# Four convolution layers on one core: a coupled map in two halves of three channels instead of three pairs, with other orders of work around it

## The chip, the cores and the metric

The kernel runs on one core of a Trainium2 chip. The time is the device time of one execution, in microseconds (us). Three runs of the kernel before took 16,030.44, 16,057.42 and 16,071.58 us, median 16,057.42. One more execution was recorded by the hardware profiler.

The engines are named as the profile names them: PE (TensorE, matrix multiplications into PSUM), PEld (its weight loads), DVE (VectorE), ACT (ScalarE), POOL (GpSimd, which here issues DMAs), SP (SyncE, which issues DMAs too). DVE and ACT read PSUM and empty it.

## What is computed

The input is 32 pictures of 8 channels of 256 x 256 in float32. Four layers follow one another; each adds to x something computed from x normalized over groups of two channels (_gn).

```
drive = grid = gn(x)                                   # layer 0
for _ in range(15):                                    # "the map", "the automaton"
    mapped = 3.9 * grid * (1 - grid)
    local  = conv3x3(mapped, K_local, one kernel per channel)
    grid   = 0.85 * (0.7 * mapped + 0.3 * local) + 0.15 * drive
cml = clip(grid, 0.0001, 0.9999)
nca = sigmoid(conv1x1(relu(conv3x3(gn(x), Wp)), Wu))   # 8 -> 128 -> 8 channels
g   = sigmoid(conv1x1(relu(conv3x3([gn(x), cml, nca], Wg1)), Wg2))   # "the gate"
x   = x + g * cml + (1 - g) * nca
x   = x + conv3x3(quantized gn(x), quantized weight) / scales + bias     # layer 1
x   = x + conv3x3(gn(x), weight) + bias                                  # layer 2
x   = x + mean over 5x5 of gn(x), per channel                            # layer 3
```

## The kernel before, in words

**Layer 0 is one long pass over the 32 pictures.** Three generators are woven into one order of instructions by hand, in one loop: lattice() makes the map of one picture, errands() loads and normalizes the next picture, and gated() makes the hidden convolution and the gate. lattice() yields numbers, the "gaps"; the loop draws so much work from gated() as fills each gap (gated() yields what its pieces cost, in about the same unit), as long as the batch that gated() has reached (place[0]) stays under a cap (place[1]). The cap keeps the hidden convolution of a picture a few batches short of the point up to which its inputs are written: these are the batches held back, which are then drawn in the next picture's opening.

**The map.** Six of the eight channels (CP = 6) run on PE, the last two as nine shifted multiply-adds on DVE. For PE a channel lies as a tile of 128 partitions (16 blocks of rows x 8 columns within a block) by 512 elements. One step of one channel is two matmuls into one PSUM bank: `patch_sb` times the channel's state (L408), which covers the neighbours inside the patch, and `ring_sb` times `rings` (L410), which covers the neighbours beyond its border. `rings` is filled from the state by DMAs from SBUF to SBUF: spread() issues them on SP (L272). Then DVE adds the drive (L418), ACT squares the result into the state (L435), and the cycle begins again. ps_c holds three PSUM banks for these sums.

Before the change, channels go in pairs (j, 3 + j) for j = 0, 1, 2. The ring of a channel has 56 rows; the ring of the first of a pair lies on partitions 0 to 55 (LOW), that of the second on 64 to 119 (HIGH), so that two ring matmuls of 56 rows use different rows of the array. Two sets of tiles exist: pairs 0 and 1 are spread together after pair 1, pair 2 alone. A spread is 6 DMAs for each of the two sides, so 12; a step has 24.

The two channels on DVE lie in `strip`, 4 rows with one row above and below. tap(dy, dx) is one multiply-add of 128 x 1024 (L342), nine a step: two after pair 0, three after pair 1, four after pair 2, in the order dy = 1 first. Then L428 and L429 form the next values, and edges() fetches the rows above and below by two DMAs on SP (L278, L279). work(4) draws four of the gate's DVE operations (L603 to L612) from a list, `spare`, once a step; next(ahead) draws a piece of errands().

**The hidden convolution and the gate.** A batch is four matmuls `ph` of a 72-row input `im` (L684), each emptied by ACT into `hh` (L689), and four small matmuls `pn` (L661) which run side by side. A picture has 32 batches. `im` has four buffers; six DMAs on POOL (L540) fill one. The gate takes eight rounds a picture: POOL loads its inputs (L557, L494, L499, L562), PE makes eight matmuls of 128 x 128 and two of 72 x 32 (L571, L579, L583), ACT makes relu and sigmoid (L585, L590) with a matmul between them (L588), and DVE's seven operations go to `spare`. pieces() draws a stage of each gate at the end of each batch.

PSUM tiles of ph, of the small statistics (L109, L116, L138, L329), of the transposes (L366, L450) and of L588 share one ring of three banks.

**Layers 1 to 3** are a second pass, one picture at a time through all three: in one turn of its loop layer 3 of picture b - 3 runs first (eight parts, into which among() puts statistics, the quantization of picture b and the normalization normal2() of picture b - 1), then both() runs layer 2 of picture b - 1 and layer 1 of picture b, one part of each in turn. The copies beside() and beside3() (SP, L148, L860) bring rows of neighbouring blocks next to one another before the convolutions.

Of the kernel before, what the change touches and what calls it, by code (L numbers as in the profile page):

```python
# [17 lines left out]
P = 128  # L18
# [9 lines left out]
PW = 8  # L28
# [11 lines left out]
    (32, 8, (RB - 1) * PW, 1, -1, 1, 0),  # L40
    (40, 8, 0, 1, 1, 1, 0),
    (48, 2, (RB - 1) * PW, PW - 1, -1 - SY, 2, 2 * SY),
    (52, 2, 0, PW - 1, 1 - SY, 2, 2 * SY),
)
RING = 56
LOW, HIGH = 0, 64
# [3 lines left out]
PAIRS = CP // 2  # L50

SETS = ((0, 2), (2, 1))
RQ = 4
BLOCK = 12.6
# [17 lines left out]
def kernel(  # L72
# [59 lines left out]
    def by_group(psum, st):  # L132

        sel = small.tile([P, 4, 2], F32, name="sel")
        for j in range(2):
            nc.vector.tensor_scalar(sel[:, :, j], gsel_sb, st[:, j : j + 1], None, ALU.mult)
        ps = psum.tile([P, 512], F32, name="ps")
# [3 lines left out]
        return got  # L141
# [31 lines left out]
    with ExitStack() as es:  # L173
        wt = es.enter_context(tc.tile_pool(name="wt0", bufs=1))
        imp = es.enter_context(tc.tile_pool(name="im", bufs=4))
# [7 lines left out]
        ring_sb = const(wt, ring, [P, PAIRS, P], "ring_sb")  # L183
# [33 lines left out]
        for c in range(CP):  # L217
# [9 lines left out]
        states = [  # L227
            [wt.tile([P, k, SN], F32, name=f"state{i}_{side}") for side in range(2)]
            for i, (_, k) in enumerate(SETS)
        ]  # L230
        rings = [wt.tile([P, k, SN], F32, name=f"rings{i}") for i, (_, k) in enumerate(SETS)]
# [6 lines left out]
        for t in (*states[0], *states[1], *rings):  # L238
            nc.gpsimd.memset(t, 0.25)
# [15 lines left out]
        def inner(c):  # L255

            side, j = divmod(c, PAIRS)
            i = j // 2
            return states[i][side][:, j - SETS[i][0], AT : AT + TX * SY].rearrange(
                "p (x y) -> p x y", y=SY  # L260
            )[:, :, 0:TY]

        def spread(i):

            long = (SETS[i][1] - 1) * SN + RN
            to = rings[i].rearrange("p c n -> p (c n)")
            for state, base in zip(states[i], (LOW, HIGH)):
                row = state.ap[0][0]
                for q, n, p, step, far, m, by in RINGS:
                    at = p * row + AT + far  # L270
                    dims = [[step * row, n]] + ([[by, m]] if m > 1 else []) + [[1, long]]
                    nc.sync.dma_start(  # L272
                        to[base + q : base + q + n * m, 0:long], window(state, at, dims)
                    )
# [57 lines left out]
        def lattice(b, ahead):  # L332
# [67 lines left out]
            for step in range(STEPS):  # L400
                for j in range(PAIRS):
# [22 lines left out]
                    for dy, dx in taps_of[j]:  # L424
                        tap(dy, dx)
# [679 lines left out]
```

## Time and profile before

| | |
|---|---|
| median of three runs | 16,057.42 us (16,030.44 to 16,071.58) |
| the profiled execution | 16,044.26 us |
| its span in the profile | 16,042.5 us |
| PE busy | 15,001.2 us, 94% |
| DVE busy | 11,572.5 us, 72% |
| ACT busy | 5,754.6 us, 36% |
| POOL busy | 5,667.6 us, 35% |
| DMA: bytes and mean rate | 2,248.19 MB, 140 GB/s |
| mean granted clock of PE | 0.96 of full speed |
| layer 0 | to about 13,200 us |
| layers 1 to 3 | from about 13,320 us on |

How to read it: a line of PE's groups has line, engine, operation, tiles, shapes and count, then busy time and mean ns of one, then idle time of the engine just before these instructions and what ended it. A line of the timeline has start, duration, engine, line, operation, count, and in brackets the idle time before it with its releaser. A float32 matmul stands as two records, so L408 has 32 x 15 x 6 x 2 = 5,760. Matmuls overlap and their ends are modelled: the pace of PE is read from start to start, not from durations.

### The profile page before, as it was taken

To read this page: it belongs to the slowest core of one execution; us is meant where nothing else is said; L and a number is where in the kernel's file an instruction comes from. 1 tells how busy PE (TensorE), PEld (TensorE's weight loads), DVE (VectorE), ACT (ScalarE), POOL (GpSimd) and SP (SyncE) were. 2 spreads that over 40 slices of the span, in tenths; PEclk is the share of its full clock that TensorE was granted. 3 is DMA by queue.
4 is the path that set the end of the run, shared out by engine and by line. 5 is a ranking of instruction groups with operands and counts; after the bars stand their busy time and mean duration, and the time that the engine had idled before them with its cause. 6 is when DMAs were issued, how large, how long until landed. Compare 5 with 4: busy or idle time off the path is not lost. (4 is left out here: it accounts for less than half of the span.)

```text
span 16042.5 us, 158554 instructions
## 1 busy us (share of the span) xinstructions
PE 15001.2 (94%) x42888; PEld 5437.6 (34%) x42888; DVE 11572.5 (72%) x14652; ACT 5754.6 (36%) x8864; POOL 5667.6 (35%) x9558
## 2 busy tenths in 40 slices
PE   7999999999999999999999999999999997999999
PEld 2333333333333333333333333333333333333333
DVE  7777777777777777777777777777777775555554
ACT  3444444444434444444434444444444431111110
POOL 3433333333433433334433333333333332111111
PEclk9999999999999999999999999999999998999999
DMA  5666666666666666666666666566656554555554
GB/s 128 149 148 148 148 146 144 146 147 147 149 146 145 150 144 148 147 147 150 146 144 145 143 146 148 141 149 145 146 145 145 142 143 106 119 117 119 120 118 106
DMA packets 1172088, 2248.19 MB, mean 140 GB/s; under 512 B 472477, under 2 KB 676373, under 8 KB 1164949
## 3 DMA queue, kind: packets, MB, share of 16 engines
q0 software_dynamic: 734208, 1628.10, 42.8%
q1 hardware_dynamic: 437012, 609.95, 15.8%
q8 instruction: 370, 6.06, 0.2%
q14 instruction: 498, 4.07, 0.1%
HBM read 1169.35 MB, written 539.02 MB: 106 GB/s over the span
## 5 line engine op out<-in xcount | busy, mean ns | idle before, releaser
L342 DVE SCALAR_TENSOR_TENSOR acc<-strip,taps_sb,acc 128x1024 f32<-128x1024 f32 x3840 | 4925.9, 1283 | 485.2 <-DMA strip<-strip 387.4
L540 POOL DMA_DIRECT2D im<-xn_d x6144 | 3483.8, 573 | 4640.2 <-PE ph L684 3775.8
L684 PE MATMUL ph<-im,wp_sb 72*128 72x512 f32 x8192 | 4269.2, 635 | 269.3 <-ACT hh L689 126.5
L689 ACT ACTIVATE hh<-ph,bp_sb 128x512 f32<-128x512 f32 x4096 | 2758.0, 688 | 3778.2 <-PE ph L684 3726.1
L418 DVE SCALAR_TENSOR_TENSOR psc<-psc,flat 128x512 f32<-128x512 f32 x2880 | 1871.5, 693 | 2524.4 <-PE psc L410 2517.8
L408 PE MATMUL psc<-state,patch_sb 128*128 128x512 f32 x5760 | 2931.1, 623 | 163.0 <-ACT state L435 157.6
L435 ACT ACTIVATE state<-psc,minus 128x512 f32<-128x512 f32 x2688 | 1723.7, 689 | 3137.9 <-DVE psc L418 2756.2
L684 PEld LDWEIGHTS ph<-im,wp_sb 72*128 72x128 f32 x8192 | 1439.8, 195 | 2677.8 <-issue 1971.7
L410 PE MATMUL psc<-rings,ring_sb 56*128 56x512 f32 x5760 | 1805.7, 650 | 230.9 <-DMA rings<-state 212.6
L408 PEld LDWEIGHTS psc<-state,patch_sb 128*128 128x128 f32 x5760 | 1041.7, 194 | 1904.1 <-issue 1249.6
L871 PE MATMUL psv<-xr,w_sb 128*128 128x512 f32 x2560 | 1163.0, 600 | 1.3 <-DVE xr L852 1.3
L661 PE MATMUL pn<-hh,wu_sb 128*32 128x512 f32 x8192 | 1138.1, 624 | 0.0
L836 POOL DMA_DIRECT2D x_d<-x x512 | 324.9, 650 | 1944.5 <-DVE x L830 1703.1
L410 PEld LDWEIGHTS psc<-rings,ring_sb 56*128 56x128 f32 x5760 | 485.4, 187 | 1436.0 <-issue 1037.1
L571 PE MATMUL pg<-cq,wg_sb 128*128 128x512 f32 x1536 | 772.8, 642 | 0.0
L785 PE MATMUL psv<-xh,w_sb 128*128 128x512 f32 x1536 | 750.1, 627 | 9.6 <-issue 9.6
L571 PE MATMUL pg<-xq,wg_sb 128*128 128x512 f32 x1536 | 741.7, 620 | 0.0
L814 ACT ACTIVATE x<-psv,b_sb,sc 128x512 f32<-128x512 f32 x256 | 199.0, 777 | 1461.6 <-PE psv L789 1440.9
L562 POOL DMA_DIRECT2D xc<-xr_d x256 | 145.7, 569 | 1554.5 <-DVE ext L603 673.2
L871 PEld LDWEIGHTS psv<-xr,w_sb 128*128 128x128 f32 x2560 | 466.1, 189 | 610.9 <-issue 606.0
L342 DVE SCALAR_TENSOR_TENSOR acc<-strip,taps_sb,d 128x1024 f32<-128x1024 f32 x480 | 612.4, 1276 | 0.0
L891 DVE TENSOR_TENSOR y<-psv,y 128x512 f32<-128x512 f32 x256 | 177.1, 692 | 591.8 <-PE psv L871 591.8
(165 smaller groups left out, 12207.9 us busy)
## 6 DMA issues: line engine op xcount, KB each, us to landing
im<-xn_d POOLq DMA_DIRECT2D x6144, 96.6 KB, 4.4
rings<-state SPq DMA_DIRECT2D x1920, 70.1 KB
strip<-strip SPq DMA_DIRECT2D x960, 126.0 KB
rings<-state SPq DMA_DIRECT2D x1920, 35.1 KB
xn_d<-xb POOLq DMA_DIRECT2D x128, 516.0 KB, 11.3
nh_d<-nh POOLq DMA_DIRECT2D x256, 258.0 KB, 5.4
nr_d<-xb POOLq DMA_DIRECT2D x128, 516.0 KB, 7.0
xq<-nr_d POOLq DMA_DIRECT2D x128, 516.0 KB, 5.7
```

The lines of the kernel that those rows point to most:

```text
L342: nc.vector.scalar_tensor_tensor(acc, strip[:, dy : dy + RQ, dx : dx + W], taps_sb[:, 3 * dy + dx : 3 * dy + dx + 1], d2 if dy == 1 and dx ...
L408: nc.tensor.matmul(pss[-1], patch_sb[:, c, :], inner(c), start=True, stop=False)
L410: nc.tensor.matmul(ps, ring_sb[base : base + RING, j, :], rings[i][base : base + RING, j - SETS[i][0], 0 : TX * SY].rearrange("p (x y) -> ...
L418: nc.vector.scalar_tensor_tensor(ps, ps, FLOOR, dr[:, c], ALU.max, ALU.add)
L435: nc.scalar.activation(inner(c), ps, AF.Square, bias=minus)
L540: nc.gpsimd.dma_start(im[24 * dy : 24 * dy + 24, k, 0:run], window(xn_d[b % 3], at, [[HP * WP, C], [1, 3], [1, run]]),)
L571: nc.tensor.matmul(o, wg1_sb[:, s, dx, :], src[:, :, dx : dx + W], start=s == dx == 0, stop=False,)
L661: nc.tensor.matmul(pn[32 * q : 32 * q + 32, :], wu_sb[:, i, :], hh, start=i == 0, stop=i == 3,)
L684: nc.tensor.matmul(ph.rearrange("p (k w) -> p k w", w=W), wp_sb, im[:, :, j * WP : j * WP + W], start=True, stop=True,)
L689: nc.scalar.activation(hh, ph, AF.Relu, bias=bp_sb)
L785: nc.tensor.matmul(o, w[:, dx, :], src[:, 2 * i : 2 * i + 2, dx : dx + W], start=dx == 0, stop=False,)
L871: nc.tensor.matmul(pss[k].rearrange("p (c w) -> p c w", w=W), w3_sb[:, dx, :], xr[:, k, mine, dx : dx + W], start=dx == 0, stop=stop,)
```

## The change

It has five parts.

1. **The map in halves.** Channels 0 to 2 and 3 to 5 form two halves. Each half has one state tile and one `rings` tile. A half makes three patch matmuls, then three ring matmuls; the ring has 80 rows instead of 56 (the two DMAs of each edge and its corners become one DMA of 24 rows that overlap in the source) and is no longer placed in two row groups of the array. spread() issues 4 DMAs a half, 8 a step. Taps: the three of dy = 1 in half 0, the six of dy = 0 and 2 in half 1. work(4) stands in half 0, follow() in half 1. The gaps become 1.7 and 4.5 a half.
2. **Batches held back.** The cap lies five, not four, under the end of the picture; for the first picture it is raised only after its first squares, and a gap after the first spread is 8 instead of 5.5.
3. **Buffers and the place of the gate.** `im` has three buffers instead of four and is loaded three batches ahead instead of four; pieces() runs after the second matmul of a batch instead of at its end.
4. **Layers 1 to 3.** The steps of the statistics of layer 1 stand at parts 0, 1, 1, 2 of layer 3 instead of 0 to 3, and normal2() at part 2 instead of 3; those of layer 2 stand one part later; by_group() is split, DVE's part at part 4 and PE's at part 6, instead of both at 5; the quantization stands at parts 0, 2, 2, 3, its copy beside() at 3 instead of 4. both() starts layer 1 two parts after layer 2 and finishes it alone.
5. **Clearing.** Of the tiles cleared ahead of layer 1, DVE clears only the borders or the small ones, and POOL one (xr2), where POOL cleared six whole tiles.

The diff, cut to its core:

```diff
-    (32, 8, (RB - 1) * PW, 1, -1, 1, 0),
-    (40, 8, 0, 1, 1, 1, 0),
-    (48, 2, (RB - 1) * PW, PW - 1, -1 - SY, 2, 2 * SY),
-    (52, 2, 0, PW - 1, 1 - SY, 2, 2 * SY),
+    (32, 8, (RB - 1) * PW, 1, -1 - SY, 3, SY),
+    (56, 8, 0, 1, 1 - SY, 3, SY),
 )
-RING = 56
-LOW, HIGH = 0, 64
+RING = 80
...
-        imp = es.enter_context(tc.tile_pool(name="im", bufs=4))
+        imp = es.enter_context(tc.tile_pool(name="im", bufs=3))
...
-        ring_sb = const(wt, ring, [P, PAIRS, P], "ring_sb")
+        ring_sb = const(wt, ring, [RING, CP, P], "ring_sb")
...
+        def spread(half):
+
+            long = (HALF - 1) * SN + RN
+            state = states[half]
+            row = state.ap[0][0]
+            to = rings[half].rearrange("p c n -> p (c n)")
+            for q, n, p, step, far, m, by in RINGS:
+                at = p * row + AT + far
+                dims = [[step * row, n]] + ([[by, m]] if m > 1 else []) + [[1, long]]
+                nc.sync.dma_start(to[q : q + n * m, 0:long], window(state, at, dims))
...
-                    place[1] = BATCHES * (b + 1) - (4 if b + 1 < B else 1)
+                        place[1] = BATCHES * (b + 1) - (5 if b + 1 < B else 1)
...
-            yield 5.5
-            taps_of = (((1, 0), (1, 1)), ((1, 2), (0, 0), (0, 1)), ((0, 2), (2, 0), (2, 1), (2, 2)))
+            yield 8
             for step in range(STEPS):
-                for j in range(PAIRS):
-                    i = j // 2
-                    mine = (j, PAIRS + j)
+                for half in range(2):
+                    mine = range(HALF * half, HALF * half + HALF)
...
-                    for dy, dx in taps_of[j]:
-                        tap(dy, dx)
+                    for dy in (1,) if half == 0 else (0, 2):
+                        for dx in range(3):
+                            tap(dy, dx)
...
-                    yield 0.8
+                    yield 1.7
                     if step < STEPS - 1:
-                        for c, ps in zip(mine, pss):
-                            nc.scalar.activation(inner(c), ps, AF.Square, bias=minus)
-                        if j == SETS[i][0] + SETS[i][1] - 1:
-                            spread(i)
-                        if end:
+                        for c in mine:
+                            nc.scalar.activation(inner(c), pss[c % HALF], AF.Square, bias=minus)
+                        spread(half)
+                        if half == 1:
                             edges()
-                    if end:
+                    if half == 0:
                         work(4)
                     else:
-                        next(ahead, None)
-                    if j == 1:
                         follow()
-                    yield BLOCK - 4.0 if end else 0.8
+                    next(ahead, None)
+                    yield BLOCK - 1.7
...
                         if j == 1 and late:
                             second()
                             yield 1.05
+                        if j == 1:
+                            yield from pieces(batch)
                         yield 0.87
...
-                    yield from pieces(batch)
                     batch += 1
-                    coming = load(n + 1, i) if n + 1 < B * NCH else iter(())
+                    ahead = divmod(batch + 2, 4)
+                    coming = load(*ahead) if ahead[0] < B * NCH else iter(())
...
-                    for _ in layer2(b - 1, x2s[b - 1], bns[1]) if 1 <= b <= B else range(8):
-                        next(ones_, None)
+                    twos = layer2(b - 1, x2s[b - 1], bns[1]) if 1 <= b <= B else iter(range(8))
+                    for i, _ in enumerate(twos):
+                        if i > 1:
+                            next(ones_, None)
                         yield
+                    for _ in ones_:
+                        pass
```

BLOCK, the sum of a half's two gaps, is 6.2; before, a step's gaps summed to 12.6.

## The prediction

> **What bounds the kernel now.** I read the page's busy table, the table by stretch of the span, TensorE's groups, the waits, and the timeline of single steps. First, the busy table and two stretches (columns: stretch, PE, PEld, DVE, ACT, POOL busy, granted clock, DMA share, GB/s):
>
> ```profile
> PE 15001.2 (94%) x42888; PEld 5437.6 (34%) x42888; DVE 11572.5 (72%) x14652; ACT 5754.6 (36%) x8864; POOL 5667.6 (35%) x9558
> 4000.00:8000.00 4000.00, 3784.99 (x11025) 1329.06 (x11021) 3027.74 (x3563) 1637.58 (x2546) 1587.12 (x2720) 0.96 0.61 147
> 13600.00:15800.00 2200.00, 2068.16 (x5447) 865.65 (x5446) 1268.26 (x2315) 287.21 (x378) 359.98 (x511) 0.98 0.52 119
> ```
>
> TensorE is the bound in both parts. Layer 0 lasts to about 13,200 us (412 a picture). There TensorE is idle 786 us (13,200 less the busy time of the stretches, 12,414). A mean clock of 0.96, where the records know only 0.5 and 1.0, is 8% of the time at half speed, so 4%, 530 us, is lost. Idle and half clock cost 1,316 us, **41 us a picture**. Next, TensorE's groups in layer 0 and two waits of layers 1 to 3:
>
> ```profile
> L684 PE MATMUL ph<-im,wp_sb 72*128 72x512 f32 x8192 | 4269.2, 635 | 269.3 <-ACT hh L689 126.5 <-ACT gt L590 103.2 <-DMA im<-xn_d 21.4
> L408 PE MATMUL psc<-state,patch_sb 128*128 128x512 f32 x5760 | 2931.1, 623 | 163.0 <-ACT state L435 157.6 <-DVE flat L421 2.3 <-DMA strip<-strip 0.5
> L410 PE MATMUL psc<-rings,ring_sb 56*128 56x512 f32 x5760 | 1805.7, 650 | 230.9 <-DMA rings<-state 212.6 <-issue 17.4 <-DMA im<-xn_d 0.5
> L138 PE MATMUL ps<-sel,ones 128*128 128x8 f32 x64 | 12.6, 270 | 45.5 <-DVE sel L136 45.5
> L789 PE MATMUL psv<-qb,w_bf 72*128 72x512 bf16 x256 | 101.4, 396 | 123.1 <-DMA qb<-qh 123.1
> ```
>
> A matmul is two records. L408 and L410 have the same count and mean, but L410 is busy 1,806 instead of 2,931 us: the rings of two channels run side by side. The timeline shows the pace from start to start:
>
> ```profile
> 4006.28 2.74 PE L571 MATMUL pg<-xq,wg_sb 128*128 128x512 f32 x6
> 4008.86 1.88 PE L408 MATMUL psc<-state,patch_sb 128*128 128x512 f32 x4
> 4010.67 1.13 PE L410 MATMUL psc<-rings,ring_sb 56*128 56x512 f32 x4
> 4011.73 1.13 PE L588 MATMUL pq<-g,wg_sb 128*128 128x512 f32 x2
> ```
>
> Six plain records take 2.58 us, 0.43 each; the four of a ring pair take 1.06. The pair's surroundings pay too: 1.81 for four L408 instead of 1.72, and L588's two take 0.96 (next start 4012.69) instead of 0.86.
>
> Where the 41 us arise, by two places of the timeline. At each picture's start the rings come late, and what follows runs at half speed (3.78 us for four records):
>
> ```profile
> 4147.25 1.12 PE L410 MATMUL psc<-rings,ring_sb 56*128 56x512 f32 x2
> 4154.69 2.04 PE L410 MATMUL psc<-rings,ring_sb 56*128 56x512 f32 x2 [6.32 <-DMA rings<-state]
> 4156.66 3.78 PE L684 MATMUL ph<-im,wp_sb 72*128 72x512 f32 x4
> ```
>
> And inside the steps VectorE waits for the two edge rows of its strip, ScalarE for VectorE, TensorE for PSUM that ScalarE has not emptied:
>
> ```profile
> 3856.45 2.60 DVE L342 SCALAR_TENSOR_TENSOR acc<-strip,taps_sb,acc 128x1024 f32<-128x1024 f32 x2 [5.66 <-DMA strip<-strip]
> 3862.13 1.29 ACT L435 ACTIVATE state<-psc,minus 128x512 f32<-128x512 f32 x2 [10.93 <-DVE psc L418]
> 3864.05 3.78 PE L684 MATMUL ph<-im,wp_sb 72*128 72x512 f32 x4 [5.66 <-ACT gt L590]
> ```
>
> The waits give VectorE 387 us in 140 such stops.
>
> **What the Trainium skill says.** "TensorEngine Tiling (Array Packing)", Key Properties: tiles work in parallel, and "Changing tiling mode (not just tile) drains the TensorE". The trace agrees: 1.06 us for two ring matmuls, about 0.2 us lost around each pair. "TensorE: Matmul & The Clock Gate", What's actually happening: an idle window of about 3.4 us halves the clock; the trace shows it after the 6.32 us. The same page, Architectural detail: ScalarE and VectorE are strict first-in first-out; the chain above shows it. "DMA: Bandwidth & Descriptors", Issuing engines are not separate DMA queues: all queues share 16 engines, so larger ring transfers compete with POOL's loads (0.61 busy now); no run shows yet by how much.
>
> **The change, part by part.**
>
> *Unpacked rings.* Now one pair costs 4 x 0.43 + 0.09 + 1.06 + 0.10 = 2.97 us, three pairs 8.9 a step. After it, 80 rows need the whole array: 6 channels x 4 records x 0.43 = 10.3, without switches. That is +1.4 us in each of 15 x 32 = 480 steps: **+670**, fully on the path. Bounds: +620 (a switch costs 0.03 more than I read) to +810 (the 0.10 behind each pair is not won back).
>
> *Fewer ring DMAs.* SP issues 24 a step at 0.69 us (13.15 us for 19) and 2 strips, 18 us of a 22 to 24 us step; after it 8 and 2, some 7. Rows grow from 2 x 56 x (4.5 + 2.2 KB) to 2 x 80 x 6.8 KB, 0.75 to 1.09 MB a step, +160 MB on the page's 2,248: DMA share +0.04. The first half is ready after 3 squares and 4 issues instead of 4 and 12: 0.6 + 8 x 0.69 = 6 us sooner, and its rings are used 2.5 us later (waits of 8 instead of 5.5). The 6.3 us go, with the half clock behind them. A second half waits for 3 more squares and 4 issues, 4.7 us, and is used 11 us later: nothing, unless the transfers slow down.
>
> *Halves, centre row first.* Taps dy=1 need no edge rows and now stand in half 0; edge rows are used only in half 1, about 11 us after their issue instead of 4. The 5.66 us was a landing some 8 us after issue, so nearly all 387 us go. What comes late next is VectorE itself: half 1 has 3 x 0.61 + 6 x 1.31 + 0.72 + 1.17 = 11.6 us, half 0 has 1.8 + 3.9 + four helper operations of 0.71 = 8.6, and 0.7 a step of statistics: 20.9, of which a normal step of TensorE (10.3 + 12.4 of other work) hides all: 22.7. Where a gate flushes four more (2.8 us), VectorE is 1 to 3 us over. A half's three PSUM banks are needed 6.2 + 5.1 us after its start; VectorE then has 2 us of slack. I take 4 us a picture, bounds 0 and 15.
>
> *Amounts held back and gaps.* The gaps that lattice() yields sum to 222.8 instead of 223.3 a picture (5 + 8 + 3 + 4.8 + 8 + 15 x 12.4 + 8), so the other work of TensorE is moved, not changed. One more batch is left for the turn of pictures, 8 ph records and 8 pn records, about 4.5 us: cost nothing, since it only changes place; without it the transposes there would wait bare for VectorE and ScalarE.
>
> *Three input buffers instead of four, gates amid a batch.* The lead of a load in the built program's order falls from 34 to 23 us at the median. Moved past on POOL: the gate's 10 to 13 DMAs (0.57 us each) with their wait for VectorE. In the trace of before, 77 of 1,020 loads landed later than one batch before their use, 378 us in sum; as loads now precede the gate in the queue, I take 2 us a picture, bounds 0 and 12.
>
> *Left per picture:* 4 + 2, 1.5 for small statistics matmuls (L116 in the steps now), 3 at the turn of pictures, and half clock in the present proportion (530 to 786), some 4: **15 instead of 41**, -26 x 32 = **-830**. Bounds 8 and 26.
>
> *Layers 1 to 3.* Layer 1 begins two rounds (about 7 us) later and its edge copy a round earlier, against a wait of 123/32 = 3.8 us: gone. The group sums are split: 45 us mostly gone. With the half clock of these waits (0.98: 2% of half speed, 1% of 2,700, some 30 to 50 us) and the start, where POOL clears tiles for 20 us before it loads: **-200**, bounds -90 and -280. Two tail rounds of layer 1 cost VectorE 1.4 us each, hidden by layer 3's first 3.4 us of matmuls.
>
> **Sum.** 16,042.5 + 670 - 830 - 200 = 15,683 of span; the profiled run is 1.8 above its span, and the median of the runs 13 above that: **15,700**.
>
> **Rivals.** Differences under 0.3% (48 us) can't be told from none.
> - *Forecast*, 8 to 23 us left per picture: 15,480 to 15,950. Chance 0.55.
> - *Nearly no stall* (5 us left, -10 x 32): 15,380. For: SP and strip waits have a clear cause. Against: gates are bursts. 0.12.
> - *Only the picture starts heal* (about 27 left: some 4 us of rings, some 7 of half clock, little else goes): 15,700 + 12 x 32 = 16,080, spread 15,950 to 16,200. For: ScalarE stays behind VectorE. 0.16.
> - *Loads late* (the full 12 us a picture instead of 2, +320, and up to as much half clock again): 16,020 to 16,340. For: POOL was blocked by a gate in the late cases. Against: the queue's new order. 0.05.
> - *Slower: VectorE's half 1.* If its chunk exceeds TensorE's 11.4 us by more than the 2 us of slack, the squares come late, the banks are not free and TensorE stops in each step. At 1 us a step the picture's rest is 30 instead of 15 and the time 16,180; if all 41 us stay, it is 16,530. It decides from 26 us left on. For: 92% occupancy of VectorE. 0.12.
>
> Faster: 0.55 + 0.12 + 0.05 of the third; same 0.10 (0.08 and 0.02); slower 0.18. The range reaches down into the second case and up to the third and the edge of the last: 15,400 to 16,150.
>
> **What would show it.** L410: records 0.43 apart, busy near 2,900, no wait over 50 us in all; no first-ring wait; DVE's wait for strip under 60; L684's waits for ScalarE under 130; L789 and L138 without theirs; granted clock 0.97 to 0.98 in layer 0; about 407 us from picture to picture. It is wrong if L408 waits for L435 or DVE is over 92% busy in the steps, or L684 waits for im.

## The result, and the profile after

The kernel after took **16,744.57 us** (median of four runs, 16,739.85 to 16,758.92), the kernel before, beside it, 16,047.08 (four runs, 16,030.44 to 16,071.58). The ratio is **1.0444**, 95% interval 1.0429 to 1.0459: 698 us slower. The forecast was 15,700, its range ended at 16,150. The profiled execution has a span of 16,757.1 us, 714.6 above that of before.

First the busy table of the kernel after, from the page:

```profile
PE 15639.5 (93%) x42888; PEld 6260.4 (37%) x42888; DVE 11671.5 (70%) x14662; ACT 5733.7 (34%) x8864; POOL 5673.7 (34%) x9551
```

Then two stretches, one in layer 0 and one in layers 1 to 3 (columns as before: stretch, five engines, granted clock, DMA share, GB/s):

```profile
4000.00:8000.00 4000.00, 3712.95 (x10175) 1471.78 (x10174) 2842.16 (x3321) 1497.60 (x2351) 1452.46 (x2494) 0.93 0.64 146
14400.00:16500.00 2100.00, 2068.80 (x5556) 867.17 (x5554) 1269.63 (x2359) 292.95 (x382) 384.56 (x516) 1.00 0.61 128
```

Layer 0 went wrong: PE stands still more (287 us in the 4,000 instead of 215) and its clock is 0.93 instead of 0.96. Layers 1 to 3 went as meant: 1.00 instead of 0.98. The groups of PE name the new wait:

```profile
L668 PE MATMUL ph<-im,wp_sb 72*128 72x512 f32 x8192 | 4151.9, 633 | 789.4 <-DMA im<-xn_d 568.1 <-ACT hh L673 142.0 <-DVE xb L437 47.0
L393 PE MATMUL psc<-state,patch_sb 128*128 128x512 f32 x5760 | 2722.6, 609 | 32.2 <-ACT state L421 21.2 <-DVE flat L407 11.0
L395 PE MATMUL psc<-rings,ring_sb 80*128 80x512 f32 x5760 | 2635.3, 592 | 5.7 <-DMA rings<-state 5.7
L783 PE MATMUL psv<-qb,w_bf 72*128 72x512 bf16 x256 | 98.1, 383 | 10.9 <-DMA qb<-qh 10.9
L134 PE MATMUL ps<-sel,ones 128*128 128x8 f32 x64 | 9.3, 218 | 11.2 <-DVE sel L131 11.2
```

The waits that the change aimed at are gone: for `rings` 5.7 us instead of 212.6, for the squares (L421) 21.2 instead of 157.6, for `qb` 10.9 instead of 123.1. In their place L668, the hidden convolution, waits 568.1 us for its input `im`, which was 21.4 before. It happens at the same place in each picture, its opening. The timeline of PE there (start, duration; in brackets the idle time before; cut at the dots), and below it the busy time and granted clock of a stretch after the first stop:

```profile
4317.15 1.88 PE L668 MATMUL ph<-im,wp_sb 72*128 72x512 f32 x4
4324.39 3.75 PE L668 MATMUL ph<-im,wp_sb 72*128 72x512 f32 x4 [5.36 <-DMA im<-xn_d]
...
4343.80 3.75 PE L668 MATMUL ph<-im,wp_sb 72*128 72x512 f32 x4 [9.67 <-DMA im<-xn_d]
...
4407.23 3.75 PE L668 MATMUL ph<-im,wp_sb 72*128 72x512 f32 x4 [9.25 <-DMA im<-xn_d]
```

```profile
4324.39:4330.94 6.55, 6.55 (x13) 1.85 (x14) 0.00 (x0) 4.46 (x7) 5.03 (x8) 0.50 0.83 165
```

There are three stops in this picture, 24 us, and after each the same four records take 3.75 us instead of 1.88: the clock is halved (0.50 in the stretch shown). These are batches 29 and 30 of the picture that ends and batch 2 of the next; over all pictures they stop PE for 149, 239 and 169 us. What POOL, which issues the loads, does in the same time:

```profile
4302.50 4.06 POOL L343 DMA_DIRECT2D xn_d<-xb  x4 [16.75 <-DVE xb L337]
4306.56 2.24 POOL L524 DMA_DIRECT2D im<-xn_d  x4
4311.41 0.56 POOL L524 DMA_DIRECT2D im<-xn_d  x1 [2.61 <-DMA xn_d<-xb]
4314.68 0.56 POOL L524 DMA_DIRECT2D im<-xn_d  x1 [2.71 <-DMA xn_d<-xb]
4320.80 0.60 POOL L602 DMA_DIRECT2D x_d<-xc  x1 [5.55 <-DMA xn_d<-xb]
4325.37 0.56 POOL L546 DMA_DIRECT2D xc<-xr_d  x1 [3.97 <-DMA x_d<-xc]
4325.93 1.70 POOL L524 DMA_DIRECT2D im<-xn_d  x3
4327.63 2.77 POOL L462 DMA_DIRECT2D cr_d<-xb  x4
4332.14 0.58 POOL L524 DMA_DIRECT2D im<-xn_d  x1 [1.74 <-DMA xc<-xr_d]
```

POOL waits 16.75 us for DVE to normalize the next picture (L337), issues four stores of 516 KB, and after four more DMAs each further one waits for one of these stores to land, although the loads read another picture's tile. The built program's order on POOL shows why (rows in order, cut at the dots, with the semaphores that each waits for):

```
2167 L343 DMACopy xn_d_203<-xb_173 8x16x1032 [waits DMASW2_49,DVE_49]
2168 L343 DMACopy xn_d_203<-xb_173 8x16x1032 [waits DMASW3_49]
2169 L343 DMACopy xn_d_203<-xb_173 8x16x1032 [waits DMASW4_49]
2170 L343 DMACopy xn_d_203<-xb_173 8x16x1032 [waits DMASW5_49]
2171 L524 DMACopy im<-xn_d_202 24x1x1030 [waits DMASW6_49,PE_49]
...
2175 L524 DMACopy im<-xn_d_202 24x1x1030 [waits DMASW2_49]
2176 L524 DMACopy im<-xn_d_202 24x1x1030 [waits DMASW3_49]
2177 L602 DMACopy x_d_81<-xc 128x512 [waits DMASW4_49]
2178 L546 DMACopy xc<-xr_d_204 128x512 [waits DMASW5_49,DMASW4_49]
```

POOL's DMAs take eight semaphores in turn, so each waits until the one eight places ahead of it has landed. The fifth load DMA after four stores waits for the first store, the sixth for the second, x_d for the third: the brackets of the timeline, one by one. A store landed 11.1 us after its issue at the median, a load DMA 5.8. So POOL has at most eight transfers in flight, and four large ones hold up what comes eight places later.

For batch 30 these waits count: those of the timeline sum to 14.8 us before its first DMA is issued (at 4325.93), 10.9 of them for stores. For batch 29 they don't: the first four DMAs of its load were issued without a wait and yet landed 14.4 to 15.0 us after their issue (medians over the pictures; 2.8 to 3.5 for batches 27 and 28), and the last two, which had waited, landed only 0.5 us after them. That load is late because it stands behind stores that wait for DVE, and then because its transfers take so long beside theirs. The order by semaphores is the same in the kernel before, but there the loads of batches 28 to 30 are issued ahead of the stores and land 2.8 to 7.5 us after issue.

### The profile page after: what moved, and what is told of

The parts are those of the page before. It is cut to its first block, busy times and chain, and to the rows that moved or that the text cites. A ratio compares the mean times of both kernels' runs of the same rounds, so it can differ in the third digit from the quotient of the medians.

```text
span 16757.1 us, 141212 instructions
## 1 busy us (share of the span) xinstructions
PE 15639.5 (93%) x42888; PEld 6260.4 (37%) x42888; DVE 11671.5 (70%) x14662; ACT 5733.7 (34%) x8864; POOL 5673.7 (34%) x9551
## 5 line engine op out<-in xcount | busy, mean ns | idle before, releaser
L668 PE MATMUL ph<-im,wp_sb 72*128 72x512 f32 x8192 | 4151.9, 633 | 789.4 <-DMA im<-xn_d 568.1
L404 DVE SCALAR_TENSOR_TENSOR psc<-psc,flat 128x512 f32<-128x512 f32 x2880 | 1939.6, 696 | 3564.5 <-PE psc L395 3561.9
L393 PE MATMUL psc<-state,patch_sb 128*128 128x512 f32 x5760 | 2722.6, 609 | 32.2 <-ACT state L421 21.2
L395 PE MATMUL psc<-rings,ring_sb 80*128 80x512 f32 x5760 | 2635.3, 592 | 5.7 <-DMA rings<-state 5.7
L668 PEld LDWEIGHTS ph<-im,wp_sb 72*128 72x128 f32 x8192 | 1561.9, 199 | 2789.9 <-issue 2054.3
L421 ACT ACTIVATE state<-psc,minus 128x512 f32<-128x512 f32 x2688 | 1696.9, 690 | 1641.4 <-DVE psc L404 1441.1
L393 PEld LDWEIGHTS psc<-state,patch_sb 128*128 128x128 f32 x5760 | 1106.5, 195 | 1557.2 <-issue 1475.9
L395 PEld LDWEIGHTS psc<-rings,ring_sb 80*128 80x128 f32 x5760 | 1091.4, 190 | 1397.9 <-issue 1385.7
L645 PE MATMUL pn<-hh,wu_sb 128*32 128x512 f32 x8192 | 1268.8, 674 | 6.6 <-ACT hh L673 6.6
L830 POOL DMA_DIRECT2D x_d<-x x512 | 374.4, 746 | 1394.8 <-DVE x L824 1172.2
L415 DVE SCALAR_TENSOR_TENSOR strip<-acc 128x1024 f32<-128x1024 f32 x448 | 549.7, 1227 | 15.3
## 6 DMA issues: line engine op xcount, KB each, us to landing
xn_d<-xb POOLq DMA_DIRECT2D x128, 516.0 KB, 11.1
```

What stands on the lines that cost most here:

```text
L393: nc.tensor.matmul(pss[-1], patch_sb[:, c, :], inner(c), start=True, stop=False)
L395: nc.tensor.matmul(pss[c % HALF], ring_sb[:, c, :], rings[half][:, c % HALF, 0 : TX * SY].rearrange("p (x y) -> p x y", y=SY)[:, :, 0:TY], ...
L404: nc.vector.scalar_tensor_tensor(ps, ps, FLOOR, dr[:, c], ALU.max, ALU.add)
L421: nc.scalar.activation(inner(c), pss[c % HALF], AF.Square, bias=minus)
L645: nc.tensor.matmul(pn[32 * q : 32 * q + 32, :], wu_sb[:, i, :], hh, start=i == 0, stop=i == 3,)
L668: nc.tensor.matmul(ph.rearrange("p (k w) -> p k w", w=W), wp_sb, im[:, :, j * WP : j * WP + W], start=True, stop=True,)
```

## The experiments

Below, *turn* is the time from the first tap of a picture's last step to the first tap of the next picture (mean of 31), *steps* that of the 14 steps before it (mean of 32), *tail* what follows the last of these taps, and *stops* the idle time of PE, in sum, before batches whose load of `im` landed at the end of it. (The start of the kernel is left out, so that before has 6 here and 21.4 in the group above; the groups name only the last wait, so they can differ from this column by some 20 us.) All are from the traces. Times are medians; each ratio is to runs of the kernel before on the same chip. Kernels that ran on different occasions are compared by their ratios, a hundredth being 160 us.

| kernel | us | ratio, 95% interval | turn | steps | tail | stops |
|---|---|---|---|---|---|---|
| before | 16,047 | 1 | 71.3 | 339.8 | 2,869 | 6 |
| after | 16,745 | 1.0444 (1.0429 to 1.0459) | 93.6 | 344.8 | 2,727 | 582 |
| after_im3s | 16,657 | 1.0367 (1.0348 to 1.0386) | 91.9 | 342.2 | 2,725 | 556 |
| after_im4 | 16,089 | 1.0021 (1.0013 to 1.0028) | 78.9 | 338.2 | 2,724 | 123 |
| after_hold3 | 16,280 | 1.0130 (1.0108 to 1.0152) | 87.1 | 336.1 | 2,711 | 322 |
| after_gates_end | 16,457 | 1.0236 (1.0216 to 1.0257) | 91.0 | 337.0 | 2,722 | 515 |
| after_sp | 16,410 | 1.0246 (1.0220 to 1.0272) | 82.2 | 344.3 | 2,729 | 283 |
| after_sp_gates_end | 16,075 | 1.0018 (1.0010 to 1.0027) | 80.2 | 337.1 | 2,721 | 290 |
| after_im4_sp | 15,942 | 0.9937 (0.9920 to 0.9955) | 76.3 | 335.3 | 2,729 | 6 |
| after_old_order | 15,777 | 0.9823 (0.9807 to 0.9838) | 73.2 | 334.9 | 2,711 | 122 |
| old_order_sp | **15,563** | 0.9717 (0.9698 to 0.9736) | 71.7 | 329.1 | 2,707 | 14 |
| before_im3 | 16,102 | 1.0023 (1.0014 to 1.0032) | 82.2 | 330.7 | 2,861 | 217 |
| before_order | 15,850 | 0.9870 (0.9855 to 0.9885) | 72.8 | 331.7 | 2,886 | 164 |
| before_l13 | 15,890 | 0.9882 (0.9863 to 0.9901) | 70.9 | 340.7 | 2,701 | 6 |
| pairs_order_l13 | 15,661 | 0.9776 (0.9760 to 0.9792) | 72.7 | 330.5 | 2,715 | 145 |
| pairs_order_l13_sp | 15,672 | 0.9769 (0.9749 to 0.9789) | 74.3 | 329.8 | 2,714 | 118 |
| before_unpacked | 16,134 | 1.0044 (1.0026 to 1.0061) | 72.3 | 340.8 | 2,873 | 6 |
| before_6taps | 15,779 | 0.9816 (0.9801 to 0.9831) | 68.4 | 334.2 | 2,874 | 8 |
| pairs_centre | 15,972 | 0.9943 (0.9926 to 0.9960) | 73.2 | 341.1 | 2,708 | 6 |

From before to after the turns cost 31 x 22.3 = 691 us, the steps 32 x 5.0 = 160, and the tail gives 142 back. In the turns PE's idle time rose from 216 to 519 us, and the time that PE works at half clock from 168 to 834, half of which is lost: +303 and +333 of the 691. In the steps both fell (idle time 517 to 410, work at half clock 764 to 488: 245 us less), though the stops of batch 2 lie there, and yet the steps are 160 longer. So some 400 us of the steps are new work of PE, an estimate by difference: that is what unpacked rings bring.

**The fourth buffer** (after_im4), with its control (after_im3s). Room for a fourth `im` was made the same way in both; only after_im4 then uses it.

```diff
 # both
-        d2s = [wt.tile([P, RQ, W], F32, name=f"d2_{i}") for i in range(2)]
+        d2s = [wt.tile([P, RQ, W], F32, name="d2_0")] * 2
...
 # the same for nhs; d2 is loaded by SP at the map's start, not by POOL ahead; zero rows come from xn_d
 # after_im4 alone
-        imp = es.enter_context(tc.tile_pool(name="im", bufs=3))
+        imp = es.enter_context(tc.tile_pool(name="im", bufs=4))
-                    ahead = divmod(batch + 2, 4)
+                    ahead = divmod(batch + 3, 4)
```

Expected of after_im4:

> The kernel after, with four im buffers and loads four batches ahead again. To make room, d2 and nh have one buffer each and the zero row comes from memory. Theory of the loads: TensorE's 582 us of stops for im in batches 2, 29, 30 and 31 of a picture go, and with them most of the half clock at the turns that grew by 660 us (330 us of time): 15,850 us, between 15,750 and 16,000. Rival, the map in halves itself (VectorE's second half) or the held-back batches are the cause: 16,600 or more, with the turn still near 93 us.

Expected of after_im3s:

> The kernel after with the same room saved (one buffer for d2 and nh, zero row from memory) but three im buffers as it has: the control for the one with four. If saving room costs nothing, both theories expect the time of the kernel after, 16,745 us, within 60. What it differs is the price of the saving.

Measured: 16,089, slower than the 15,750 to 16,000 expected, against 16,657 for the control. So the fourth buffer alone is worth **569 us**, 17.8 a picture; making the room gave 0.8% (1.0444 to 1.0367), where nothing was expected. PE's group in after_im4:

```profile
L664 PE MATMUL ph<-im,wp_sb 72*128 72x512 f32 x8192 | 4007.1, 616 | 358.6 <-ACT hh L669 166.0 <-DMA im<-xn_d 142.5 <-DVE xb L433 47.7
```

and in after_im3s:

```profile
L664 PE MATMUL ph<-im,wp_sb 72*128 72x512 f32 x8192 | 4119.0, 630 | 744.5 <-DMA im<-xn_d 545.5 <-ACT hh L669 130.8 <-DVE xb L433 48.6
```

The wait for `im` falls by 403 us and nothing of that size takes its place; most of the rest comes with the half clock (in the turns PE works 744 us at half speed, then 499). Late loads are the larger part of the loss, but the kernel is still no faster than the kernel before.

**The other parts of the order, each undone alone** (after_hold3, after_gates_end):

```diff
 # after_hold3
-                        place[1] = BATCHES * (b + 1) - (5 if b + 1 < B else 1)
+                        place[1] = BATCHES * (b + 1) - (4 if b + 1 < B else 1)
-                    place[1] = BATCHES - 5
+                    place[1] = BATCHES - 4
 # after_gates_end
-                        if j == 1:
-                            yield from pieces(batch)
...
+                    yield from pieces(batch)
                     batch += 1
```

> The kernel after with three batches held back instead of four, three im buffers. At the normalization batch 28 instead of 27 is under way, so the slow loads serve batches 30 and 31 instead of 29 and 30. Theory of the loads: the stop of batch 29 moves to 30, that of 30 to 31, which the turn needs only late; stops fall by some 150 to 250 us with half of their half clock: 16,400 to 16,600. Rival, the held-back batches don't matter: within 80 us of 16,745.

> The kernel after with pieces() at the end of a batch again, three im buffers. Theory: in the turn the gate's DMAs and x1 stores (x_d, xc) stand between the two slow loads on POOL, and the place of the gate is what makes the second one (batch 30, lands 44 us after the normalization) late: 150 to 350 us less than the kernel after, 16,400 to 16,600. Rival, only the count of buffers and of batches held back matters: within 80 us of 16,745.

Each gives back much: 3.1% with three held back, more than expected, and 2.1% with gates at the end. With three held back the stop at batch 2 is gone (169 to 14 us); batches 30 and 31 still stop PE for 300. The steps fall as well, 344.8 to 336.1 us a picture. With gates at the end the time lies in the expected range, but by luck: the stops that were to go hardly move (582 to 515), and the gain lies in the steps, 344.8 to 337.0. So part of the loss does not go through late loads.

**The same parts in the pairs** (before_im3: three buffers alone; before_order: three buffers, four held back, gates amid a batch). The edits are those above, made in the kernel before.

> The kernel before with three im buffers and loads three batches ahead, nothing else. Theory of the loads: one buffer less alone brings the stops at the turn: 500 to 900 us more than before, 16,550 to 16,950. Rival, it is the map in halves or the fourth batch held back that makes the loads late: less than 150 us more, under 16,200.

> The kernel before with the pairs, but with three im buffers, gates amid a batch and four batches held back, as in the kernel after: the parts that move the loads, without the map in halves and without the new layers 1 to 3. Theory of the loads: these three together cost what they cost in the kernel after (some 800 us), whatever the map is: 16,650 to 16,950. Rival, the loads are late only because halves run the other work in longer stretches: 16,100 to 16,350.

Three buffers alone cost the pairs 0.23%: the turns grow by 10.9 us, with 217 us of stops, but the steps shrink by 9.1. All three moves together make the pairs *faster*, 0.987. My theory, that these parts are harmful by themselves, fell here. POOL in before_order at a picture's opening:

```profile
4083.66 4.05 POOL L356 DMA_DIRECT2D xn_d<-xb  x4 [3.12 <-DVE xb L350]
4087.70 1.68 POOL L540 DMA_DIRECT2D im<-xn_d  x3
4089.38 0.61 POOL L618 DMA_DIRECT2D x_d<-xc  x1
4102.64 0.56 POOL L562 DMA_DIRECT2D xc<-xr_d  x1 [12.65 <-DMA x_d<-xc]
4103.21 3.36 POOL L540 DMA_DIRECT2D im<-xn_d  x6
4106.56 2.09 POOL L478 DMA_DIRECT2D cr_d<-xb  x3
```

The same stores stand here too, but POOL waits 3.12 us for DVE, not 16.75, half of a load is out before them (3 of its DMAs follow, in the kernel after all 6), and the next load's six DMAs stand ahead of the four cr_d stores, in the kernel after only its first three do. Its loads 29 and 30 landed 21.0 and 30.5 us after the normalization's start and were used at 21.2 and 31.0; in the kernel after they landed at 23.9 and 44.1. (All are medians over the pictures.) The harm is in how the pieces meet, not in any one of them.

**The large stores off POOL's queue** (after_sp): the four xn_d and four cr_d DMAs of a picture's opening are issued on SP.

```diff
-                nc.gpsimd.dma_start(
+                nc.sync.dma_start(
                     window(
                         xn_d[b % 3], (1 + r) * WP,
...
-                nc.gpsimd.dma_start(
+                nc.sync.dma_start(
                     window(
                         cr_d[b % 3], r // 4 * C * HB * WP,
```

> The kernel after, all parts as they are (three im buffers, gates amid a batch, four held back), but the eight large DMAs of a picture's opening (xn_d from xb, cr_d from xb) are issued on SP instead of POOL. Theory: POOL's queue stands behind these eight, each of its later DMAs waiting until they land, and the two im loads that stand there (batches 29 and 30) are what TensorE waits for: then most of the 582 us of stops and half of their clock go: 15,950 to 16,300. Rival: the DMA engines themselves are full in the opening, or gate inputs block batch 2: over 16,500.

1.0246 instead of 1.0444, some 320 us less, with three buffers and everything else as in the change: 16,410, between the theory's range and the rival's. PE's group:

```profile
L668 PE MATMUL ph<-im,wp_sb 72*128 72x512 f32 x8192 | 4092.9, 626 | 525.9 <-DMA im<-xn_d 297.9 <-ACT hh L673 170.2 <-DVE xb L437 47.8
```

The wait for `im` halves: batch 29's stop is gone, batch 30's falls from 239 to 130 us, batch 2's stays (146). That the stores stood in the loads' way is shown. The Trainium skill ("DMA: Bandwidth & Descriptors", Issuing engines are not separate DMA queues) says that all transfers run on the same 16 engines and that issuing from another engine saves only the sequencer's time. Here it saved more: 320 / 32 = 10 us a picture, where the eight issues take POOL 4.06 + 2.77 = 6.8. What is saved besides are POOL's waits, for stores eight places ahead and for DVE in front of the stores: the load of batch 29 now begins 0.3 us after its buffer is free instead of 6.3, that of batch 30 9.2 instead of 17.3 (medians). The transfers are shorter too: the second to fourth DMA of load 29 land 9.6 to 10.6 us after issue instead of 14.4 to 15.0. The same page (SWDGE vs HWDGE vs iDMA) has POOL's and SP's DMAs feed different internal queues of an engine, between which it takes turns; that fits, but no run here separates it from other traffic at the changed moment.

**Batch 2 and the gates** (after_sp_gates_end: both edits above).

> The kernel after with the eight large DMAs of a picture's opening on SP and, besides, the gate's inputs yielded at the end of a batch instead of amid it; three input buffers and four batches held back stay. With the large DMAs alone moved, batch 2 of a picture still stopped TensorE for 146 us and batch 30 for 130 us in sum. If the gate's 12 input DMAs are what batch 2 stands behind, its 146 us go and the time is 16,220 to 16,300. If batch 2 is late because the lead of three buffers is too short there, whatever the gate does, its stop stays and the time is 16,350 to 16,420, less only what gates at the end gain elsewhere (the earlier run, without the moved DMAs, gained 287 us with batch 2's stop nearly unchanged).

Batch 2's stop stays, 154 us, so putting the gate's inputs half a batch later does not heal it. But the test was weaker than I had thought: in its trace the load of batch 2 still stands behind them on POOL, and behind an x_d store that waits 7.93 us for DVE. In the kernel after it is alike: POOL waits 10.08 us for DVE before such a store and 10.4 us more between the gate's input DMAs. Which of these makes batch 2 late is not settled; three held back (above) or a fourth buffer heal it. The ratio, 1.0018, is 2.3% below that of after_sp, and the time below both ranges, though the stops are the same: again the gates' place is worth some 300 us that do not go through late loads.

**Loads on time, order as in the change** (after_im4_sp) and **order as before** (after_old_order: four buffers, gates at the end, three held back; old_order_sp: these and the stores on SP). The edits are those above, combined.

> The kernel after with four input buffers and the eight large DMAs on SP; four batches held back and gates amid a batch stay as in the change. If late loads are nearly the whole loss, no load stops TensorE and the time is within 1% of the fastest so far, 15,563: 15,560 to 15,720. If holding back four batches and the place of the gates cost something of their own beyond late loads, it stays above 15,800.

> The map in halves with 80-row rings and the new layers 1 to 3, but four im buffers, gates at the end of a batch and three batches held back as in the kernel before (with one buffer for d2 and nh, to make room). Theory: the order of the loads was the whole loss, and the map in halves by itself is no slower than the pairs: at or under the pairs with the new layers 1 to 3 (15,890), 15,650 to 15,900. Rival, unpacked rings cost their TensorE time once the stops are gone: 16,000 or more.

> The fastest so far (halves, four im buffers, gates at the end, three held back: 15,777) with the same eight DMAs on SP. Its stops for im are 122 us in all, so by the theory there are 50 to 200 us to win: 15,580 to 15,730. Rival, its loads are ahead enough: within 40 us.

after_im4_sp has 6 us of stops left and yet takes 15,942. old_order_sp, which differs only in three instead of four held back and gates at the end, is 2.2% lower, 15,563, just under what was expected of it; their spans, 15,922.5 and 15,559.1, are 363 us apart. after_old_order lies in its range. "Late loads are nearly the whole loss" fell. Where these 363 lie: PE's groups of after_im4_sp,

```profile
L664 PE MATMUL ph<-im,wp_sb 72*128 72x512 f32 x8192 | 3977.5, 612 | 241.5 <-ACT hh L669 166.9 <-DVE xb L433 48.1 <-DMA rings<-state 18.9
L111 PE MATMUL ps<-t,gavr_sb 128*128 128x1 f32 x192 | 31.2, 232 | 60.9 <-DVE t L108 60.9
```

and of old_order_sp:

```profile
L664 PE MATMUL ph<-im,wp_sb 72*128 72x512 f32 x8192 | 4085.5, 611 | 206.7 <-DVE u L112 79.8 <-DVE xb L433 40.5 <-ACT hh L669 39.3
L111 PE MATMUL ps<-t,gavr_sb 128*128 128x1 f32 x192 | 27.9, 214 | 8.6 <-DVE t L108 8.6
```

PE's idle time is 134 us smaller (595 to 461), mostly waits of the hidden convolution for ACT (166.9 to 39.3) and of small statistics matmuls for DVE (60.9 to 8.6), partly replaced by others (L112, 79.8); the time that PE works at half clock falls from 755 to 360, which is about 200 more. That fits bursts which ACT and DVE cannot follow, but it is not shown, and no run separates the two moves here. old_order_sp is the fastest kernel of the study, 2.8% below the kernel before. A stretch of its layer 0 (columns as above):

```profile
4000.00:8000.00 4000.00, 3936.99 (x11400) 1579.09 (x11399) 3184.57 (x3716) 1670.46 (x2634) 1558.45 (x2705) 0.99 0.72 164
```

PE is idle 63 us in 4,000 and its clock is 0.99.

**The terms of the sum, by themselves.** before_unpacked: the kernel before with ring matmuls one after the other on all 128 rows. before_l13: with the new layers 1 to 3. before_6taps: three of the nine taps are left out, so that the two channels on DVE compute another map. pairs_centre: before_l13 with the row dy = 1 first.

```diff
 # before_unpacked (ring_sb has one weight a channel, zero on the other channel's rows)
-                    for ps, base in zip(pss, (LOW, HIGH)):
+                    for c, ps in zip(mine, pss):
                         nc.tensor.matmul(
-                            ps, ring_sb[base : base + RING, j, :],
-                            rings[i][base : base + RING, j - SETS[i][0], 0 : TX * SY].rearrange(
+                            ps, ring_sb[:, c, :],
+                            rings[i][:, j - SETS[i][0], 0 : TX * SY].rearrange(
 # before_6taps
-            taps_of = (((1, 0), (1, 1)), ((1, 2), (0, 0), (0, 1)), ((0, 2), (2, 0), (2, 1), (2, 2)))
+            taps_of = (((1, 0), (1, 1)), ((1, 2), (0, 0)), ((0, 1), (0, 2)))
 # pairs_centre
-            taps_of = (((1, 0), (1, 1)), ((1, 2), (0, 0), (0, 1)), ((0, 2), (2, 0), (2, 1), (2, 2)))
+            taps_of = (((1, 0), (1, 1)), ((1, 2),), ((0, 0), (0, 1), (0, 2), (2, 0), (2, 1), (2, 2)))
```

> The kernel before with ring matmuls of 128 rows, one after the other (the weights of the other channel's rows are zero, so the result is the same), spread and all else as before; the zero row comes from memory. By the sum of the prediction each step takes 1.4 us more of TensorE: +670 if it is all on the path, 16,720. Rival, TensorE's idle time in the steps (517 us in all) takes it up: +150 to +350, 16,200 to 16,400.

> The kernel before with layers 1 to 3 and their clearing as in the kernel after, layer 0 unchanged. The traces have this part at 2,869 us before and 2,727 after, 142 us less: 15,905 us, 15,870 to 15,950. Rival, the gain came from how layer 0 ends: less than 60 us.

> The kernel before with six of the nine taps of the two channels on VectorE: the three of dy = 2 are left out, so these two channels are another map. 3.9 us of VectorE's 20.9 us a step go, TensorE's work is the same. Theory: VectorE (with its wait for the strip) paces the steps, and TensorE's idle time and half clock in the steps (517 us and half of 635 us) are what it waits for VectorE; then most of these 834 us go: 15,300 to 15,700 us. Rival: TensorE's own work bounds the steps or the rings' transfers do: less than 150 us, over 15,900.

> The kernel before with the new layers 1 to 3 and the taps in another order: dy = 1 in pairs 0 and 1, all six of dy = 0 and 2 in pair 2, so that the edge rows are used later. If VectorE's wait for the strip (387 us in 140 stops) costs TensorE time, it is 50 to 250 us under the 15,890 of the pairs with the new layers 1 to 3. Rival, the longer chunk of pair 2 (9.8 us with psc) delays the next pair 0 as much: within 40 us, or over.

*before_unpacked* cost 0.44%, some 70 us, less than either expectation, where the prediction had +670. Its two groups of the map and a stretch of layer 0:

```profile
L407 PE MATMUL psc<-state,patch_sb 128*128 128x512 f32 x5760 | 2812.7, 607 | 50.2 <-ACT state L434 48.5 <-DVE flat L420 1.5
L409 PE MATMUL psc<-rings,ring_sb 128*128 128x512 f32 x5760 | 2803.4, 610 | 319.5 <-DMA rings<-state 294.4 <-issue 20.3 <-DMA strip<-strip 4.2
```

```profile
2000.00:13000.00 11000.00, 10574.76 (x30223) 4182.16 (x30222) 8387.82 (x9816) 4526.76 (x6982) 4317.71 (x7411) 0.98 0.61 146
```

The same stretch of the kernel before:

```profile
2000.00:13000.00 11000.00, 10393.22 (x30269) 3652.39 (x30270) 8330.92 (x9836) 4497.60 (x6993) 4326.66 (x7417) 0.96 0.61 146
```

The added work is there: over layer 0, PE's idle time fell by 198 us (733 to 535) and the time at half clock by 530 (1,038 to 508), so 198 + 265 + 70, at most some 530 us, are new work, 1.1 us a step. But it takes the place of idle time and half clock. In the pairs, the packing saved PE time for which PE then stood waiting. *before_l13* gave 1.18%, some 190 us. *before_6taps* gave 1.84%, some 300 us, between the two expectations: DVE's taps do stand on the path of the kernel before, for a part of its waits. *pairs_centre* is 0.6% slower than before_l13: with the pairs, ending DVE's waits for the strip was worth nothing when six taps came last, since PE's waits for the squares grew instead (155 to 305 us) and those for rings too (210 to 275).

**Do the halves win?** (pairs_order_l13: the pairs with three buffers, four held back, gates amid a batch and the new layers 1 to 3; pairs_order_l13_sp: and the stores on SP.)

> The pairs with three im buffers, gates amid a batch and four held back (15,850) and the new layers 1 to 3 as well, which took 170 us off the pairs before: 15,680, 15,640 to 15,730. It says what the map in halves alone costs beside pairs, with all other parts of the kernel after: the difference to 16,745.

> The kernel before (three pairs, packed rings) with the change's three input buffers, four batches held back, gates amid a batch and layers 1 to 3, and the eight large DMAs on SP. It is the pairs' counterpart of the fastest kernel with halves (15,563). If halves with the centre row first are worth nothing beyond what the order of loads gives, the two are equal within 50 us: 15,510 to 15,610. If halves win some 100 us by ending the waits for strips and rings, this run stays at 15,600 to 15,680, little below its 15,661 without the moved DMAs, as it had no late loads but 145 us.

0.9776, as expected, and 0.9769: moving the stores does nothing for the pairs. The halves' best is 0.5% below, some 80 us, but 118 us of stops at batch 30 are left in the pairs' run. pairs_order_l13 also shows what the map in halves costs with all other parts as in the change: 1.0444 instead of 0.9776. Four ratios side by side, all with the new layers 1 to 3:

| | order as before (four buffers, gates at the end, three held back) | order as in the change |
|---|---|---|
| pairs | 0.9882 (before_l13) | 0.9776 (pairs_order_l13) |
| halves | 0.9823 (after_old_order) | 1.0444 (after) |

Neither the halves nor the order is the loss by itself; the two together are. (after_old_order holds the making of room besides, which is worth 0.0077 from after to after_im3s, so whether halves beat pairs by themselves stays open.)

## Why the prediction was wrong, point by point

- **"Three input buffers instead of four, gates amid a batch ... I take 2 us a picture, bounds 0 and 12"**: the step that failed first. The third buffer costs 17.8 us a picture (after_im3s to after_im4), above the upper bound. I judged the lead by its median over the whole picture, "from 34 to 23 us". In the opening PE has no map to compute, so the batches of the hidden convolution follow one another sooner: where their loads are in time, batches 29 and 30 start 8.5 and 9.2 us after the batch before them (after_im4, means), against 417 / 32 = 13.0 on the mean, while the queue that loads them holds eight large stores. The upper bound took the landing times of the kernel before and moved only the deadline, by one batch. But the landings moved too: the DMAs of load 29 land 2.8 to 3.9 us after issue in the kernel before and 9.7 to 15.0 in the kernel after (medians), since they now come behind the stores. "As loads now precede the gate in the queue" looked at the gate and not at the stores.
- **"Amounts held back and gaps ... cost nothing, since it only changes place"**: failed too. With the loads on time, this and the gates' place cost 363 us (after_im4_sp to old_order_sp), 11.3 a picture.
- **"+670" for the unpacked rings**, "fully on the path": too large. As an estimate, take the span less PE's idle time and less half of the time that PE works at half clock. By this the new work is 518 us in before_unpacked, 1.1 us a step instead of 1.4, and 448 to 484 us, about 1.0 a step, in the kernels with halves. In the pairs it was not on the path: idle time and half clock made room for it, and the kernel took 70 us more.
- **"15 instead of 41", -830**: by the same measure idle time and half clock in steps and turns rose by 391 us in the kernel after, 12 a picture, because loads came late and the order cost more. In old_order_sp they fell by 781, 24 a picture: near the forecast, but with the order of work that the change gave up, and the stores on SP. How much of the 781 are waits that healed, and how much is new work in the place of waiting, as in before_unpacked (459 us less), no run separates; the prediction added its two terms as if they were independent. Its sum has a slip as well: half clock "in the present proportion (530 to 786)" of 10.5 us is 7 us and not "some 4", which makes some 80 us.
- **Ring DMAs and centre row**: right in the trace. The rings' wait is 5.7 us, DVE's wait for `strip` 8.5 instead of 387 ("under 60"), six ring records take 2.57 us from start to start, 0.43 each. What they are worth was not shown by pairs_centre.
- **Rival "VectorE's half 1"**, my case on the slow side: wrong. In the steps DVE is busy 82% of the time (before 80%), where its sign was 92%, and L393 waits for the squares 21.2 us in all.
- **"Loads late", 16,020 to 16,340, chance 0.05**: the right mechanism at too small a price. It had 12 us of stops a picture, where 582 / 32 = 18 were measured, and nothing for what the order costs when loads are on time.
- **Layers 1 to 3, -200**: right within its bounds. The tail is 142 us shorter, before_l13 gives some 190.
- **Granted clock "0.97 to 0.98"**: 0.93 in the stretch shown; with 6 us of stops in all, in after_im4_sp, it is 0.98 in the same stretch.

The way from the kernel after to one within the forecast range, in measured ratios: 1.0444 less 0.0077 (room), 0.0346 (fourth buffer) and 0.0198 (gates at the end, three held back) is 0.9823, 15,777 us. The wait "L684 waits for im", which the prediction named last as a sign of its own failure, is the one that showed it.

## What to carry to other kernels

Judge a prefetch by its smallest lead, at the place where its consumer runs fastest, and write out the queue that issues it there: every large transfer in that queue, and how many it keeps in flight. Don't add a cost of work and a saving of waits on the same engine as if they were independent: in the pairs, 518 us of added work cost 70, since PE stood still for a part of the time. If several parts of an order change at once, try them together and alone, since what harms one version helped the other.

## What was not expected of the hardware

- A stop of 5.36 us on PE made the next four records take 3.75 us instead of 1.88, as did stops of 9.67 and 9.25. The clock stayed at 0.50 for 6.6, 11.0 and 5.6 us of work after them, half of which is lost: an estimate of 3 to 5 us a stop beyond its own length.
- Eight DMAs of a picture, moved from POOL to SP, gave some 320 us in the kernel after (1.0444 to 1.0246), and nothing in the pairs.
- PE time saved by packing two ring matmuls side by side (1.1 us a step) came back almost whole as idle time and half clock: undoing it cost 0.44%.
